# Fewer, larger transfers around the second layer of a graph network: kept rows by pairs, slot numbers by groups, segment marks by a product with a 0-1 matrix

## The chip, the core and the metric

The kernel runs on one core of a Trainium2 chip. Its time is the device time of one execution in microseconds (us); the time before is a median over four runs. Profile rows name the engines PE (TensorE matmul), PEld (its weight loads), DVE (VectorE), ACT (ScalarE), POOL (GpSimd) and SP (SyncE); SPq is SP's queue of transfers. In this kernel every plain transfer of the two long loops is issued by SP, in program order, and every indirect gather by POOL, in program order.

## The reference

A graph of 6250 nodes with 256 features and 106250 edges, sorted by destination; each node has one edge to itself. There are two layers, each followed by a residual and a layernorm.

```python
# layer 0
msgs = relu(relu(S @ W_r.T + b_r) @ W_r.T + b_r)       # S = feat[src], r = the edge's relation (0 or 1)
agg  = segment_sum(msgs, dst)
i, f, g, o = split(agg @ W_ih.T + b_ih + b_hh, 4)
hn   = sigmoid(o) * tanh(sigmoid(i) * tanh(g))
x    = layernorm(x + relu(relu(hn @ W1.T + b1) @ W2.T + b2) @ W3.T + b3)
# layer 1, four heads of 64 features
h    = (x @ W).reshape(n, 4, 64)
e    = leaky_relu(a_src[src] + a_dst[dst], 0.2)
ex   = exp(e - segment_max(e, dst)[dst])
out  = segment_sum(h[src] * ex / (segment_sum(ex, dst)[dst] + 1e-16), dst) + bias
x    = layernorm(x + relu(layernorm(out + x) * gamma + beta))
```

The inputs are those of `setup_inputs()`: float32 features and weights, int32 indices.

## The kernel before

**Tiling.** The self edges are taken out of the list, which leaves 100000 edges in TC = 782 tiles of P = 128. Seven tiles (WT) make a window (112 of them); the destinations of a window fit in 64 node slots. Two windows make a group (NG = 56), whose 128 slots fill the 128 partitions. Layer 1 works on pairs of groups: groups 0 to 51 in 26 pairs, the last four alone. Layer 0 does its update for two pairs (four groups) at a time up to group 47, then for pairs and for single groups.

**Layer 0.** The two-layer edge network depends on the source node and the relation only, so it is computed once for each node and relation and stored to DRAM (`parts`). For each tile POOL gathers 128 of these rows (helper `gather`, L1720), and PE sums them by slot with a one-hot matrix (L2162). `update()` (L1976 to L2127) then does the gates, the three-layer network, the residual and the layernorm of its groups, projects the result to `h` with the attention terms (`hr`, L2090), and writes two things to DRAM through SP: the rows that layer 1 gathers (L2097, two stores per group), and for each group a tile of 128 x 768 floats (`keep3`: projected rows, a copy made by ACT at L2091, and what layer 1's end needs), stored as `kept` at L2107. `keep3` is a ring of six tiles.

**Layer 1.** The first 21 tiles (EARLY) need rows that are not yet stored when they are gathered; `complete()` adds them by a one-hot product (L2272 to L2285). For the others POOL gathers rows from `rows`, up to a look-ahead that is largest at the start of the layer and shrinks to eight tiles (AHEAD1): `Pace.hold` lets a gather wait for a given DVE instruction. For each pair:

- `ahead()` (L2292 to L2342) loads with SP the slot number of every edge, broadcast from a DRAM table over the 64 partitions of each half (`dB`, L2301, two transfers of 128 KB for each group), and the segment marks (`cut`, L2308, one transfer of 30 KB for each group: 60 partitions of 129 floats, in which each tile's row stands four times, once for each head). Eight steps later it compares dB with the partition's own number (`ohT`, L2315), multiplies with the node terms (`pn`, L2319) and reduces (`of`, L2336).
- `weights()` (L2344 to L2397) adds, turns the logits on PE (L2359), runs segmented scans on DVE in which `cut` holds the bounds (L2366 and L2367), brings together segments that cross tiles (L2370 to L2374, with ACT's copy `ends` at L2372), scans again, turns back (L2382) and takes the exponential. PE's turns and small products share a ring of two PSUM buffers, `turn`.
- `weighted()` (L2399 to L2416) builds the one-hot tiles (L1826) and the weighted rows (L2405, L2410, L2411), and `sum1()` (L2498 to L2528) sums them on PE (L2526). At a group's first tile it loads the group's kept rows (`k3`, L2516, a ring of three).
- `finish()` (L2418 to L2491) divides, applies both layernorms with `k3`, and stores the output (L2477).

**What sets the order.** The program is written out by hand: functions are chains that yield a number of steps (class `Steps`), the main loop (L2547 to L2587) moves each chain on by one step per tile, and so the order on each engine and in each queue is the order of these steps. `aheads()` (L2530) starts `ahead()` of a pair about one pair before `weights()` of it, so its loads go out in SP's queue beside stores of outputs and loads of kept rows.

Of the kernel before, what the change touches and what calls it, by code (L numbers as in the profile page):

```python
# [33 lines left out]
F32 = mybir.dt.float32  # L34
# [8 lines left out]
P = 128  # L43
# [39 lines left out]
BLOCK1, BLOCK2 = 33, 40  # L83
AHEAD_G = range(AHEAD_W // 2)
LATE = 3
AHEAD0 = 2 * WT
AHEAD1 = WT + 1
NOROW = NP + SLOTS - 1
# [656 lines left out]
def gnn_kernel(  # L745
# [47 lines left out]
    slots = dram.tile([NW, (WT + 1) * P], BF16, name="slots")  # L793
    cuts = dram.tile([(NC + 1) * CT, P], F32, name="cuts")
    srcs = dram.tile([EARLY, P], F32, name="srcs")
    kept = dram.tile([NG, P, 3 * D], F32, name="kept")
    packed = dram.tile([2 * BLOCKS, HB], I32, name="packed")

    const = ctx.enter_context(tc.tile_pool(name="fconst", bufs=1))
# [844 lines left out]
def fast(  # L1644
# [46 lines left out]
    def at(ap, offset, dims):  # L1691
        return bass.AP(tensor=ap.tensor, offset=ap.offset + offset, ap=dims)
# [9 lines left out]
    def windows_of(g):  # L1702
        return range(2 * g, 2 * g + 2)
# [67 lines left out]
    def half_of(w):  # L1771
        return slice(SLOTS * (w % 2), SLOTS * (w % 2 + 1))
# [68 lines left out]
    with (  # L1841
# [134 lines left out]
        def update(groups, aT):  # L1976
# [62 lines left out]
            mv = ring(up, [P, 4, 2], F32, "fmv", 3)  # L2039
            rstd = ring(up, [P, 4], F32, "frstd", 3)  # L2040

            keep3 = [ring(up, [P, 3, D], F32, "keep3", 6) for g in groups]
            for i, g in enumerate(groups):
                u = everyone
                p3 = ring(upp, [P, 4 * P], F32, "fpg", 5)[:, : 2 * P]
# [34 lines left out]
            for i, g in enumerate(groups):  # L2080
                u = everyone
                ph = ring(upp, [P, 4 * P], F32, "fpg", 5)[:, : D + 2 * H]
                for k in range(2):
                    nc.tensor.matmul(  # L2084
                        ph[u, :], hs[i][:, k, u], Wx[:, k, :], start=(k == 0), stop=(k == 1)
                    )
                hr = ring(up, [P, D + 2 * H], F32, "hr", 3)
                if g >= NG - LATE:
                    hr = rows_l[:, g - (NG - LATE), :]
                nc.scalar.copy(hr[u, :], ph[u, :])  # L2090
                nc.scalar.copy(keep3[i][u, 2, :], ph[u, :D])  # L2091

                in_order(stored, g)
                for w in windows_of(g):
                    if w in at_w:
                        to = rows1[bass.ds(at_w[w], SLOTS), :]
                        keep_row(g, nc.sync.dma_start(to, hr[half_of(w), :HA]))  # L2097
                if g == NG - 1:
                    move = nc.gpsimd.indirect_dma_start(
                        out=rows1,  # L2100
                        out_offset=bass.IndirectOffsetOnAxis(ap=tail_i, axis=0),
                        in_=hr[:, :HA],
                        in_offset=None,
                    )
                    keep_row(g, move)
                yield 1
                nc.sync.dma_start(kept[g, u, :], keep3[i][u, :, :].rearrange("p c f -> p (c f)"))  # L2107

                nd = ring(up, [P, 2, H], F32, "nd", 3)
                left = ring(up, [P, 2, H], F32, "left", 3)  # L2110
                nd3 = ring(up, [P, 3, 2, H], BF16, "nd3", 3)
                nc.vector.tensor_copy(nd[u, 0, :], hr[u, HA : HA + H])  # L2112
                nc.vector.tensor_copy(nd[u, 1, :], hr[u, D:HA])
                lg = loop[u, g, :]
                nc.vector.tensor_add(lg, nd[u, 0, :], nd[u, 1, :])
                n3 = [nd3[u, c, :, :] for c in range(3)]
# [12 lines left out]
        got, ohs, sums, turned, stored, loop0, rows_x = {}, {}, {}, {}, [], {}, {}  # L2129
        run.start(weights_of_logits())  # L2130

        def order_of(g):
# [113 lines left out]
    with (  # L2246
# [40 lines left out]
        def tiles_in(g):  # L2287

            t0 = 2 * WT * g
            return range(t0, min(t0 + 2 * WT, TC)), range(t0, min(t0 + GS, TC))  # L2290

        def ahead(pair, box):  # L2292

            cut = ring(ep, [P, P + 1], F32, "cut", 3)
            of = ring(ep, [P, 2 * GS, 2 * H], F32, "of", 3)
            box.update(cut=cut, of=of)
            dBs = []
            for g in pair:
                dB = ring(ep, [P, W8, P], BF16, "dB", 3)
                for w in windows_of(g):  # L2300
                    nc.sync.dma_start(  # L2301
                        dB[half_of(w), :, :].rearrange("p j e -> p (j e)"),
                        at(slots, w * W8 * P, [[0, SLOTS], [1, W8 * P]]),
                    )
                dBs.append(dB)
            for i, g in enumerate(pair):
                n = len(tiles_in(g)[1])
                nc.sync.dma_start(  # L2308
                    cut[i * GS * H : (i * GS + n) * H, :],
                    at(cuts, tiles_in(g)[0][0] * P, [[P, n], [0, H], [1, P + 1]]),  # L2310
                )
            yield 8
            for i, (g, dB) in enumerate(zip(pair, dBs)):
                ohT = ring(ep, [P, W8, P], BF16, "ohT", 2)
                nc.vector.tensor_scalar(ohT, dB, slot_p, None, op0=OP.is_equal)  # L2315
# [26 lines left out]
                yield 1  # L2342

        def weights(pair, box):  # L2344
# [10 lines left out]
                return ap.rearrange("p (t h) -> p t h", h=H)  # L2355

            yield 1
            pe = ring(tps, [P, P], F32, "turn", 2)
            nc.tensor.transpose(pe[:rs, :], ef, ident)  # L2359
            yield 1  # L2360
            s1 = ring(ep, [P, P], F32, "s1", 2)
# [7 lines left out]
            pd = ring(tps, [P, P], F32, "turn", 2)  # L2369
            nc.tensor.matmul(pd[:rs, 0:1], toward[:rs, 0, :rs], b[:, P - 1 : P], start=True, stop=True)  # L2370
            nc.tensor.matmul(pd[:rs, 1:2], toward[:rs, 1, :rs], b[:, 0:1], start=True, stop=True)
            nc.scalar.copy(ends[:rs, :], pd[:rs, 0:2])  # L2372
# [8 lines left out]
            pm = ring(tps, [P, P], F32, "turn", 2)  # L2381
# [36 lines left out]
        def finish(g, ps):  # L2418
# [1 line left out]
            u = everyone  # L2420
            n = u.stop
            at_w = lows_of(ws)
            k3 = k3s[g]
            sm = ring(fp, [P, 4, H], F32, "sm", 3)
            w_own, den = sm[u, 0, :], sm[u, 1, :]
            nc.vector.tensor_sub(w_own, loop[u, g, :], ps[u, HA:])
# [71 lines left out]
        def sum1():  # L2498
# [12 lines left out]
            if g not in sums:  # L2511
                sums[g] = ring(eps, [P, D + 2 * H], F32, "fps1", 2)
                left[g] = len(tiles_in(g)[1])
                u = everyone
                k3s[g] = ring(fp, [P, 3, D], F32, "k3", 3)
                nc.sync.dma_start(k3s[g][u, :, :].rearrange("p c f -> p (c f)"), kept[g, u, :])  # L2516
            begins = left[g] == len(tiles_in(g)[1])
            left[g] -= 1
            j = t - 2 * WT * g
# [14 lines left out]
                yield from ahead(pair, boxes[pair[0]])  # L2534


        shift = ep.tile([P, 2, P], F32, name="shift")
        own_q = ep.tile([P, 2], F32, name="own_q")
        nc.vector.tensor_scalar(own_q, own_n[:, LATE - 2 :], float(N - P), None, op0=OP.subtract)
        for q in range(2):  # L2540
            nc.vector.tensor_scalar(
                shift[:, q, :], iota_f, own_q[:, q : q + 1], None, op0=OP.is_equal
            )
        run.start(aheads())
        pace = Pace(0)
        t = 0
# [103 lines left out]
```

## Time and profile before

| what | value |
|---|---|
| median of four runs | 2797.2 us (2789.18 to 2802.23) |
| profiled execution | 2816.18 us, span 2814.4 us, mean granted clock of TensorE 0.747 |
| layer 0's even part | about 200 to 1500 us of the span |
| layer 1's even part | about 1582 to 2790 us of the span |
| stores of kept rows | 56 of 384 KB |
| loads of kept rows | 56 of 384 KB |
| loads of slot numbers | 112 of 128 KB |
| loads of segment marks | 56 (55 of 30.2 KB, one of 24.2 KB) |

A row of the profile's first part reads: engine, busy us, share of the span, instructions. A group's row reads: line, engine, operation, output and input names, shapes, count, then busy us and mean ns of one, then the idle time in front of it with what ended most of that. In the chain that ended last each step leads back to what released it; "another core or an unknown queue" (or "remote") is a wait whose releaser the records do not show. A row of the waits reads: engine and line, what it waited for, us in all, times, longest us. A row of the timeline reads: start us, length us, engine, line, operation, output and input, and in square brackets the wait in front of it. A window's row reads: from and to, length, busy us and count of PE, PEld, DVE, ACT and POOL, granted clock, mean busy share of the 16 DMA engines, GB/s.

### The profile page before, as it was taken

To read this page: it belongs to the slowest core of one execution; us is meant where nothing else is said; L and a number is where in the kernel's file an instruction comes from. 1 tells how busy PE (TensorE), PEld (TensorE's weight loads), DVE (VectorE), ACT (ScalarE), POOL (GpSimd) and SP (SyncE) were. 2 spreads that over 40 slices of the span, in tenths; PEclk is the share of its full clock that TensorE was granted. 3 is DMA by queue.
4 is the path that set the end of the run, shared out by engine and by line. 5 is a ranking of instruction groups with operands and counts; after the bars stand their busy time and mean duration, and the time that the engine had idled before them with its cause. 6 is when DMAs were issued, how large, how long until landed. Compare 5 with 4: busy or idle time off the path is not lost. (4 is left out here: it accounts for less than half of the span.)

```text
span 2814.4 us, 23466 instructions
## 1 busy us (share of the span) xinstructions
PE 1574.7 (56%) x5945; PEld 822.3 (29%) x5945; DVE 1282.9 (46%) x3508; ACT 503.9 (18%) x1571; POOL 1527.9 (54%) x1610
## 2 busy tenths in 40 slices
PE   8855776575766766667744634534334342524354
PEld 5533433232322323323422412212222121212122
DVE  8542232322322322323322566755656565656576
ACT  3312021111111111112222011111111111111112
POOL 1253656665656565665544545556565655556561
PEclk9977888887878888788876756666666666656676
DMA  4333534444433443444434334435343444444441
GB/s 145 115 108 110 154 111 128 126 126 126 132 109 116 131 137 113 126 119 132 139 102 115 100 98 123 122 107 135 100 134 98 130 114 121 123 115 122 113 129 52
DMA packets 164626, 334.53 MB, mean 119 GB/s; under 512 B 42657, under 2 KB 75156, under 8 KB 164481
## 3 DMA queue, kind: packets, MB, share of 16 engines
q0 software_dynamic: 76048, 207.99, 27.5%
q1 hardware_dynamic: 86257, 121.90, 14.1%
q10 hardware_dynamic: 2176, 3.05, 0.4%
q8 instruction: 49, 0.80, 0.1%
q14 instruction: 96, 0.79, 0.1%
HBM read 280.25 MB, written 52.53 MB: 118 GB/s over the span
## 5 line engine op out<-in xcount | busy, mean ns | idle before, releaser
L1720 POOL DMA_INDIRECT G<-rows,fidx x761 | 725.7, 954 | 531.0 <-issue 160.9
L1720 POOL DMA_INDIRECT G<-parts,fidx x722 | 692.4, 959 | 487.4 <-issue 217.1
L2526 PE MATMUL fps<-gw,oh 128*64 128x264 f32 (+1 forms) x1674 | 431.8, 462 | 253.2 <-DVE gw L2411 251.7
L2162 PE MATMUL fps<-G,oh 128*64 128x257 f32 (+1 forms) x1674 | 465.0, 429 | 128.4 <-ACT G L2211 109.3
L2526 PEld LDWEIGHTS fps<-gw,oh 128*64 128x64 f32 (+1 forms) x1674 | 222.4, 164 | 419.0 <-DVE gw L2411 270.0
L2162 PEld LDWEIGHTS fps<-G,oh 128*64 128x64 f32 (+1 forms) x1674 | 204.0, 153 | 373.0 <-issue 184.2
L2411 DVE TENSOR_TENSOR gw<-G,bank 128x1792 f32<-128x1792 f32 (+1 forms) x167 | 249.0, 1491 | 63.0 <-ACT gw L2410 45.5
L2001 PE MATMUL fpg<-faT,fWihT 128*128 128x512 f32 (+2 forms) x432 | 187.1, 553 | 22.4 <-issue 16.9
L2382 PE MATMUL turn<-fident,s 120*128 120x120 f32 (+2 forms) x30 | 13.2, 439 | 294.0 <-DVE sm L2432 238.3
L2112 DVE COPY nd<-hr 128x4 f32<-128x4 f32 x53 | 9.6, 180 | 298.1 <-ACT hr L2090 226.1
L1826 DVE TENSOR_TENSOR oh<-bank,fslot 128x1024 f32<-128x1024 f32 x106 | 128.9, 1216 | 10.8 <-ACT bank L2390 6.8
L1575 PE MATMUL fpm<-fWrT,fhT 128*128 128x256 f32 x392 | 101.6, 413 | 12.2 <-DVE fms L1583 7.5
L1609 POOL DMA_INDIRECT G<-parts,fidx x60 | 57.0, 950 | 91.2 <-DMA parts<-fms 73.5
L2001 PEld LDWEIGHTS fpg<-faT,fWihT 128*128 128x128 f32 x432 | 75.4, 202 | 98.7 <-issue 88.0
L1919 DVE TENSOR_SCALAR kind<-fps 128x1 f32<-128x1 f32 x112 | 12.3, 151 | 198.8 <-PE fps L2162 173.8
L1561 PE MATMUL fph<-fxc,fWrT 128*128 128x512 f32 (+1 forms) x208 | 93.8, 600 | 10.7 <-ACT fhT L1568 5.8
L2460 ACT ACTIVATE frs<-fmv,eps_c 128x1 f32<-128x1 f32 x112 | 33.0, 294 | 360.6 <-DVE gw L2405 162.3
L2382 PEld LDWEIGHTS turn<-fident,s 120*128 120x128 f32 (+2 forms) x30 | 5.3, 177 | 298.8 <-DVE sm L2432 240.8
L1575 PEld LDWEIGHTS fpm<-fWrT,fhT 128*128 128x128 f32 x392 | 79.0, 207 | 34.8 <-issue 13.4
L2014 DVE TENSOR_TENSOR fgg<-fgg,fgi 128x512 f32<-128x512 f32 (+2 forms) x36 | 20.5, 571 | 144.5 <-ACT fgg L2009 111.0
L2466 ACT ACTIVATE fy<-fy,frs 128x256 f32<-128x256 f32 x112 | 66.8, 596 | 87.4 <-DVE gw L2405 51.0
L2084 PE MATMUL fpg<-Wx,fyT 128*128 128x264 f32 x224 | 77.1, 474 | 7.7 <-ACT fyT L2075 3.0
(347 smaller groups left out, 1993.3 us busy)
## 6 DMA issues: line engine op xcount, KB each, us to landing
kept<-keep SPq DMA_DIRECT2D x56, 384.0 KB
k<-kept SPq DMA_DIRECT2D x56, 384.0 KB
dB<-slots SPq DMA_DIRECT2D x112, 128.0 KB
loop<-parts SPq DMA_DIRECT2D x110, 128.0 KB
parts<-fms SPq DMA_DIRECT2D x49, 256.0 KB
G<-parts,fidx POOLq DMA_INDIRECT x782
G<-rows,fidx POOLq DMA_INDIRECT x761
fxn<-in_x_dram SPq DMA_DIRECT2D x110, 64.0 KB
```

The source lines that it names most:

```text
L1561: nc.tensor.matmul(ph[:, :cols], WrT_s[:, r, k, m * P : (m + 1) * P], xc[:, k, :cols], start=(k == 0), stop=(k == 1),)
L1575: made = nc.tensor.matmul(pm[:, r, :], hT[:, r, k, j * P : (j + 1) * P], WrT_s[:, r, k, :], start=(k == 0), stop=(k == 1),)
L1609: nc.gpsimd.indirect_dma_start(out=of[:, n % WT, :D], out_offset=None, in_=parts0[: 2 * P * block, :], in_offset=bass.IndirectOffsetOnAxis ...
L1720: return nc.gpsimd.indirect_dma_start(out=to_tile, out_offset=None, in_=table, in_offset=bass.IndirectOffsetOnAxis(ap=idx, axis=0),)
L1826: nc.vector.tensor_tensor(to[:, :nj, :], iota_s[:, None, :].to_broadcast([P, nj, SLOTS]), of[:, :, None].to_broadcast([P, nj, SLOTS]), op= ...
L2001: nc.tensor.matmul(pg[:, :cols], WihT_s[:, k, c * P : (c + 1) * P], aT[:, k, :cols], start=(k == 0), stop=(k == 1),)
L2084: nc.tensor.matmul(ph[u, :], hs[i][:, k, u], Wx[:, k, :], start=(k == 0), stop=(k == 1))
L2162: nc.tensor.matmul(sums[g][to, :], ohj, got[t], start=begins, stop=ends)
L2411: nc.vector.tensor_mul(gw[:, :, :D].rearrange("p j (h f) -> p j h f", h=H), of[:, :n, :D].rearrange("p j (h f) -> p j h f", h=H), ex[:, o ...
L2460: nc.scalar.activation(r, mv[u, k, 1:2], AF.Ln, bias=eps_c[u])
L2466: nc.scalar.activation(y, y, AF.Identity, bias=m, scale=r)
L2526: nc.tensor.matmul(sums[g][to, :], ohj, gw, start=begins, stop=ends)
```

## The change

Kept rows of two groups go in one transfer: the DRAM tensor `kept` gets the shape pairs x 128 x 2 x 768, so that both groups' rows of a partition lie side by side. In `update()` the ring of six tiles becomes one of three pair tiles, and the store goes out once per pair, after the odd group's row stores (56 stores become 30; the four single groups keep their own). In `sum1()` the ring of three becomes two pair tiles, loaded at the first tile of the even group (56 loads become 30).

The slot numbers of a group come in one transfer of 128 partitions, whose source has an outer step of two windows, 64 repeats and 1024 numbers (112 loads become 56).

The segment marks are loaded once, ahead of layer 1's loop: `cut_all`, 113 partitions x 7 chunks x 129 floats, row r of chunk c being tile 112 c + r (CR = 16 x 7 = 112). `pick` is a matrix of 0 and 1, 113 x 4 x 120, made by eight DVE operations. In `ahead()` PE multiplies the pair's columns of `pick` with its chunk of `cut_all`, which picks each tile's row and repeats it four times; the product goes into the `turn` ring, whose buffers become 129 columns wide, and ACT copies it to `cut`. This stands in the step that issues the loads, ahead of the `yield 8`.

```diff
-    kept = dram.tile([NG, P, 3 * D], F32, name="kept")
+    kept = dram.tile([NG // 2, P, 2, 3 * D], F32, name="kept")
...
-            keep3 = [ring(up, [P, 3, D], F32, "keep3", 6) for g in groups]
+            for g in groups:
+                if g % 2 == 0:
+                    kept_of[g // 2] = ring(up, [P, 2, 3, D], F32, "keep3", 3)
+            keep3 = [kept_of[g // 2][:, g % 2, :, :] for g in groups]
...
-                nc.sync.dma_start(kept[g, u, :], keep3[i][u, :, :].rearrange("p c f -> p (c f)"))
+                if len(groups) == 1:
+                    nc.sync.dma_start(
+                        kept[g // 2, :, g % 2, :], keep3[i].rearrange("p c f -> p (c f)")
+                    )
+                elif g % 2:
+                    nc.sync.dma_start(
+                        kept[g // 2], kept_of[g // 2].rearrange("p i c f -> p i (c f)")
+                    )
...
-                dB = ring(ep, [P, W8, P], BF16, "dB", 3)
-                for w in windows_of(g):
-                    nc.sync.dma_start(
-                        dB[half_of(w), :, :].rearrange("p j e -> p (j e)"),
-                        at(slots, w * W8 * P, [[0, SLOTS], [1, W8 * P]]),
-                    )
+                dB = ring(ep, [P, W8 * P], BF16, "dB", 3)
+                nc.sync.dma_start(
+                    dB, at(slots, 2 * g * W8 * P, [[W8 * P, 2], [0, SLOTS], [1, W8 * P]])
+                )
                 dBs.append(dB)
+            o = pair[0] % 2 * GS * H
+            n = ((len(pair) - 1) * GS + len(tiles_in(pair[-1])[1])) * H
+            pc = ring(tps, [P, P + 1], F32, "turn", 2)
+            nc.tensor.matmul(
+                pc[:n, :],
+                pick[:, pair[0] % 8 // 2, o : o + n],
+                cut_all[:, pair[0] // 8, :],
+                start=True,
+                stop=True,
+            )
+            nc.scalar.copy(cut[:n, :], pc[:n, :])
+            yield 8
             for i, g in enumerate(pair):
-                n = len(tiles_in(g)[1])
-                nc.sync.dma_start(
-                    cut[i * GS * H : (i * GS + n) * H, :],
-                    at(cuts, tiles_in(g)[0][0] * P, [[P, n], [0, H], [1, P + 1]]),
-                )
-            yield 8
-            for i, (g, dB) in enumerate(zip(pair, dBs)):
                 ohT = ring(ep, [P, W8, P], BF16, "ohT", 2)
-                nc.vector.tensor_scalar(ohT, dB, slot_p, None, op0=OP.is_equal)
+                nc.vector.tensor_scalar(
+                    ohT.rearrange("p j e -> p (j e)"), dBs[i], slot_p, None, op0=OP.is_equal
+                )
...
-            pe = ring(tps, [P, P], F32, "turn", 2)
+            pe = ring(tps, [P, P + 1], F32, "turn", 2)[:, :P]
...
-            k3 = k3s[g]
+            k3 = k3s[g // 2][:, g % 2, :, :]
...
-                k3s[g] = ring(fp, [P, 3, D], F32, "k3", 3)
-                nc.sync.dma_start(k3s[g][u, :, :].rearrange("p c f -> p (c f)"), kept[g, u, :])
+                if g % 2 == 0:
+                    k3s[g // 2] = ring(fp, [P, 2, 3, D], F32, "k3", 2)
+                of = k3s[g // 2].rearrange("p i c f -> p i (c f)")
+                if len(pair_of[g]) == 1:
+                    nc.sync.dma_start(of[:, g % 2, :], kept[g // 2, :, g % 2, :])
+                elif g % 2 == 0:
+                    nc.sync.dma_start(of, kept[g // 2])
...
+        pick = ep.tile([CR + 1, 4, 2 * GS * H], F32, name="pick")
+        for q in range(4):
+            row_q = ep.tile([P, 1], F32, name=f"row_{q}")
+            nc.vector.tensor_scalar(row_q, iota_p, float(4 * WT * q), None, op0=OP.subtract)
+            nc.vector.tensor_scalar(
+                pick[:, q, :].rearrange("p (i t h) -> p i t h", i=2, h=H),
+                bass.AP(
+                    tensor=iota_f.tensor,
+                    offset=iota_f.offset,
+                    ap=[[iota_f.ap[0][0], CR + 1], [2 * WT, 2], [1, GS], [0, H]],
+                ),
+                row_q[: CR + 1],
+                None,
+                op0=OP.is_equal,
+            )
...
+        cut_all = ep.tile([CR + 1, -(-TC // CR), P + 1], F32, name="cut_all")
+        nc.sync.dma_start(
+            cut_all, at(cuts, 0, [[P, CR + 1], [CR * P, -(-TC // CR)], [1, P + 1]])
+        )
         run.start(aheads())
```

More of the change, by code (lines that the diff above doesn't have):

```diff
@@ L85 @@
 LATE = 3
+CR = 16 * WT
 AHEAD0 = 2 * WT
@@ L2129, in fast @@
         got, ohs, sums, turned, stored, loop0, rows_x = {}, {}, {}, {}, [], {}, {}
+        kept_of = {}
         run.start(weights_of_logits())
@@ L2298, in ahead @@
             for g in pair:
-                dB = ring(ep, [P, W8, P], BF16, "dB", 3)
-                for w in windows_of(g):
-                    nc.sync.dma_start(
-                        dB[half_of(w), :, :].rearrange("p j e -> p (j e)"),
-                        at(slots, w * W8 * P, [[0, SLOTS], [1, W8 * P]]),
-                    )
-                dBs.append(dB)
+                dB = ring(ep, [P, W8 * P], BF16, "dB", 3)
+                nc.sync.dma_start(
+                    dB, at(slots, 2 * g * W8 * P, [[W8 * P, 2], [0, SLOTS], [1, W8 * P]])
+                )
+                dBs.append(dB)
+            o = pair[0] % 2 * GS * H
[10 more added lines that the diff above has]
+            yield 8
             for i, g in enumerate(pair):
-                n = len(tiles_in(g)[1])
-                nc.sync.dma_start(
-                    cut[i * GS * H : (i * GS + n) * H, :],
-                    at(cuts, tiles_in(g)[0][0] * P, [[P, n], [0, H], [1, P + 1]]),
-                )
-            yield 8
-            for i, (g, dB) in enumerate(zip(pair, dBs)):
-                ohT = ring(ep, [P, W8, P], BF16, "ohT", 2)
-                nc.vector.tensor_scalar(ohT, dB, slot_p, None, op0=OP.is_equal)
+                ohT = ring(ep, [P, W8, P], BF16, "ohT", 2)
+                nc.vector.tensor_scalar(
+                    ohT.rearrange("p j e -> p (j e)"), dBs[i], slot_p, None, op0=OP.is_equal
+                )
                 yield 2
@@ L2368, in weights @@
             yield 1
-            pd = ring(tps, [P, P], F32, "turn", 2)
+            pd = ring(tps, [P, P + 1], F32, "turn", 2)[:, :P]
             nc.tensor.matmul(pd[:rs, 0:1], toward[:rs, 0, :rs], b[:, P - 1 : P], start=True, stop=True)
@@ L2380, in weights @@
             yield slow
-            pm = ring(tps, [P, P], F32, "turn", 2)
+            pm = ring(tps, [P, P + 1], F32, "turn", 2)[:, :P]
             nc.tensor.transpose(pm[:, :rs], b, ident[:rs, :rs])
```

## The prediction

> **What bounds the kernel now.** The page comes first: no engine is near its span, and the chain that ended last holds little.
>
> ```profile
> PE 1574.7 (56%) x5945; PEld 822.3 (29%) x5945; DVE 1282.9 (46%) x3508; ACT 503.9 (18%) x1571; POOL 1527.9 (54%) x1610
> DMA  4333534444433443444434334435343444444441
> DVE 10%; another core or an unknown queue 5%; issue 3%; ACT 2%; PE 0%; POOL 0%; DMA 0%; DVEq 0%; ACTq 0%; POOLq 0%
> ```
>
> So no share of the whole decides; the stage does. The windows of layer 0 (first), the seam (second) and layer 1 (third) follow; the columns are length, then busy us (count) of PE, PEld, DVE, ACT and POOL, granted clock, DMA share, GB/s.
>
> ```profile
> 200.00:1500.00 1300.00, 868.76 (x2888) 410.03 (x2888) 379.37 (x1242) 254.57 (x660) 741.25 (x774) 0.82 0.42 123
> 1506.00:1582.00 76.00, 38.67 (x143) 29.10 (x143) 17.21 (x41) 3.32 (x10) 44.51 (x48) 0.71 0.48 133
> 1582.00:2790.00 1208.00, 495.01 (x2262) 272.03 (x2262) 744.50 (x1881) 182.55 (x765) 684.15 (x718) 0.65 0.43 116
> ```
>
> Layer 1 is where most of the change lies. It repeats once per pair of groups, at a median of 45.6 us (from the starts of the L2372 copies). Windows cut along one such period:
>
> ```profile
> 2294.90:2326.00 31.10, 16.25 (x70) 8.59 (x70) 25.62 (x63) 6.66 (x28) 18.36 (x20) 0.72 0.42 114
> 2326.00:2340.30 14.30, 1.39 (x12) 1.24 (x12) 1.38 (x6) 0.00 (x0) 8.26 (x9) 0.50 0.47 131
> 2340.30:2371.40 31.10, 16.04 (x70) 8.42 (x70) 25.58 (x63) 6.63 (x28) 18.32 (x20) 0.72 0.41 111
> ```
>
> 31.1 us are DVE's (25.6 busy, 82%). For 14.3 us PE, DVE and ACT stand still and only POOL's gathers go on. The timeline shows how that ends: ACT's copy L2372 had waited 14.35 us on a semaphore with no recorded cause. The waits of the same line give its size over the layer.
>
> ```profile
> 2340.35 0.16 ACT L2372 COPY ends<-turn 120x2 f32<-120x2 f32 x1 [14.35 <-remote]
> ```
>
> ```profile
> ACT ends L2372 <- remote: 293.8, 22, 14.8
> ```
>
> The waits of SP's own queue show what SP does meanwhile:
>
> ```profile
> SPq L2477 <- ACT gw L2410: 552.6, 25, 30.1
> SPq L2301 <- DVE G L2285: 37.5, 1, 37.5
> SPq L2516 <- DMA k<-kept: 9.4, 9, 1.4
> ```
>
> In that stand-still PE has its matmuls recorded by 2327.6, yet its semaphores come 4 to 13 us late; it ends some 2 us after the last packet of the gathers, when POOL has run out of look-ahead. I can't name the cause, only where it sits: 10 to 12 us after POOL starts to issue a gather every 1.25 us. In the first pair it comes (17.3 us) with none of SP's loads in flight, so these are not its sole cause. SP itself waits 552.6 us for values to store.
>
> **The change part by part.** The sum is made against the profiled execution (span 2814.4, time 2816.2 us) and is then moved to the median of the runs, 2797.2 us, which is 0.68% lower. Forms and rows are those of the trace.
>
> Kept rows, stores: 56 become 30 (26 pairs, four groups alone), same bytes. Each issue holds SP 0.51 us, and SP mostly waits. The even group's store now goes behind the odd group's two row stores, so behind SP's wait for ACT's L2091, met once in this trace (3.5 us); queued behind it on SP are the next groups' loads. The ring stays at six groups. Cost 0; the bounds are 6 us per double pair either way over 13 of them (periods of 84 to 91 us in layer 0 differ by about that), so -78 to +78, and I take 0 because issue and wait are near 0.
>
> Kept rows, loads: 56 become 30, the odd group's 384 KB now ride with the even group's. A 3,072-byte packet takes 121 ns; 384 KB are 8 of these on each of 16 engines, 1 us. The pair's load waits for the same finished group as the even one did. Cost 0.
>
> Slot numbers (dB): 112 transfers become 56, bytes equal. SP issues 0.60 us each, 33 us saved beside 552.6 us of waiting: 0. What matters is how the new form spreads. The old one fills 64 partitions; the new one fills 128 from a source of two outer steps with 64 repeats. The packet records of the index loads at the start of the trace show other shapes: the 126-row loads ran with up to 14 packets at once, a 125-partition one with 4.9 to 5.3, the 74-partition ones with 2.2 to 2.5. So the count of the outer step, not the bytes, sets how many engines work, and an outer step of 2 is nearest to the last row. I take 2 engines: 64 packets x 84 ns = 5.4 us for one dB, and as gathers hold about 40% of an engine at their 1.25 us spacing (0.50 us each), 5.4/0.6 = 9 us. With 2.2 us before the first packet, the pair's first dB lands about 11 us after issue, the second 20; at the pace inside the busy burst 14 and 26. The kernel before:
>
> ```profile
> 2319.28 2.42 SPq L2301 DMA_DIRECT2D dB<-slots  x4
> 2321.74 1.86 SPq L2308 DMA_DIRECT2D cut<-cuts  x2
> ```
>
> ```profile
> 2326.61 0.48 DVE L2315 TENSOR_SCALAR ohT<-dB,slot_p 128x1024 bf16<-128x1024 bf16 x1
> 2344.88 0.47 DVE L2315 TENSOR_SCALAR ohT<-dB,slot_p 128x1024 bf16<-128x1024 bf16 x1
> ```
>
> DVE uses the first dB 7.3 us after the first issue, the second 25.6 after. A first wait of 4 to 7 us falls on DVE just before the stand-still, which ends 21.1 us after issue, so it lies inside it: 0. The operations queued behind it on DVE are the scans and the one-hot products, and PE and ACT wait for those; they now wait anyway. The second is at 20 to 26 against 25.6: 0.5 us x 26 pairs = +13. Bounds: 0 if spread over 16 engines; if the cover goes, 5.5 us x 26 = +143.
>
> The Trainium skill, "DMA: Bandwidth & Descriptors", section "Why a DMA increments its semaphore by 16 and not by 1", takes the number of engines as the largest divisor up to 16 that both sides' slowest dimensions share, which speaks against this change: 2 for dB, 1 for a 113-row load. The three rows above agree (126: 14, 125: 5, 74: 2). By the rule the sum is the one below; by bytes at 16 engines it would be +5. The page's section "Rules for kernel authors" also says to coalesce small transfers into a large one; by that alone the sum would be negative by SP's issue time, and SP's 552.6 us of waiting says that nobody wants this time.
>
> Marks (cut): 56 loads of 30 KB and 0.88 us on SP go: 49 us of an idle queue, 0. In their place stands one load of 113 partitions x 7 pieces of 516 B at the seam. 113 has no divisor, so by the rows I take one engine: 791 x 33 ns = 26 us, over 0.6 = 43.5, plus 2.2: from about 1507 to 1553. It is issued ahead of dB, whose first ohT came at 1553.52:
>
> ```profile
> 1553.52 0.48 DVE L2315 TENSOR_SCALAR ohT<-dB,slot_p 128x1024 bf16<-128x1024 bf16 x1
> ```
>
> PE's new product waits for it, and the sums of the early tiles (L2278) stand behind it on PE; ACT's new copy waits for the product, and ACT's copies of e (L2571, L2579) behind that. dB of the first pair follows on its engines, to about 1562: +9. Bounds: 0 if spread, +30 at 44 ns a piece.
>
> Product and copy per pair: one fp32 matmul of 129 columns (like L2382, 0.44 us, or twice that for its greater height) and an ACT copy (0.27 to 0.37 us): 30 x 0.17 us on the path, as PE idles 3.3 us near it: +5 (0 to +20). It takes a turn more in a ring of two PSUM buffers, released by that copy. The 0-1 matrix: eight DVE operations, some 1.8 us, inside a DVE wait of 4.7 us at the seam: 0.
>
> Sum: 0 + 0 + 13 + 9 + 5 = +27: about 2843 for a profile like this one, 2824 against the median.
>
> **The rivals.**
>
> Faster: a shorter stand-still. For it: it takes 294 us on L2372 alone, follows a burst with DMA at 0.88, and was 9 us in early pairs with a deeper look-ahead. Against it: the first pair has it without SP's loads. If fewer SP transfers in that burst bring 14.4 down to 9.8, 22 x 4.6 = -101, with the seam's +9: 2705; a band of 2650 to 2788.
>
> No change: the new forms spread like the old ones, or all of it lies in the stand-still; 2797, and 2789 to 2806. The 125- and 74-partition rows speak against it; the 14.3 us of cover for it. (About 0.3% is what a measurement of this kernel can tell from none.)
>
> Slower still: dB becomes the period's bound. The mechanism is the two engines carrying dB while out and kept rows follow in the same rings; from 26 us for both dBs on it shows. 5.5 us x 26 = +143 gives 2940, half of it 2870; a band of 2870 to 2960. For it speaks the pace in the burst, against it the 40% only that gathers need.
>
> **How the numbers follow.** The forecast +27 (own range 2806 to 2870) 0.45; faster 0.30; no change 0.10; dB exposed 0.15. The range of 2700 to 2910 leaves out the lower third of the faster case (0.11) and the upper half of the last (0.08). Faster by over 0.3% is 0.30 and 0.02 of the no-change case: 0.32; within: 0.08; slower: 0.45 + 0.15 = 0.60.
>
> **What would show it.** Right: DVE's wait at L2315 is by DMA dB, several us each; dB's packets run two at a time; the first pn products come after 1555; the stand-still at L2372 shortens by as much as DVE's wait grew. Wrong: dB lands within 4 us; the period falls under 44 us with the copy's wait at 9 us; or layer 0's periods change, where I have nothing. The prediction is most at risk from the stand-still, whose cause the trace does not show.

## The result, and the profile after

The changed kernel takes 2777.95 us (median of 39 runs, 2761.36 to 2797.33) against 2796.35 us before (60 runs, 2775.28 to 2820.43). The ratio is 0.9932, with a 95% interval of 0.9918 to 0.9947: the change is faster by 0.7%, where 2824 us had been forecast.

One fact is needed for all that follows. The chips on which this was run are of two kinds. On some the kernel before takes 2772 to 2797 us and has the stand-still of 14 us in each pair that the prediction describes; on others the same program takes 2183 to 2185 us and has none. The result above, and the two profiles of this and the earlier part, are of the first kind. The experiments fell on both, and the kind is named with each; every ratio is between runs on one chip.

The page of the changed kernel, its engines and its transfers (engine, busy us, share, instructions; then line, count, size):

```profile
PE 1579.7 (57%) x6005; PEld 824.8 (30%) x6005; DVE 1283.5 (46%) x3516; ACT 510.5 (18%) x1601; POOL 1521.9 (55%) x1610
DMA packets 152063, 333.18 MB, mean 120 GB/s; under 512 B 39309, under 2 KB 69251, under 8 KB 151920
...
kept<-keep SPq DMA_DIRECT2D x26, 768.0 KB
k<-kept SPq DMA_DIRECT2D x26, 768.0 KB
dB<-slots SPq DMA_DIRECT2D x56, 256.0 KB
```

The work on the engines is that of before and the little that the change adds (60 matmul records on PE, 30 copies on ACT, eight operations on DVE), and the transfers are as few as the diff says (beside the 26 there are four of 384 KB, each way). The windows of the changed kernel, by stage and then along one pair:

```profile
200.00:1500.00 1300.00, 861.47 (x2894) 407.44 (x2894) 380.22 (x1251) 255.94 (x664) 738.75 (x775) 0.81 0.42 123
1502.00:1576.00 74.00, 33.46 (x147) 26.58 (x147) 19.30 (x51) 2.35 (x9) 44.59 (x47) 0.72 0.48 136
1576.00:2764.00 1188.00, 515.36 (x2317) 280.53 (x2317) 744.70 (x1882) 189.00 (x794) 680.26 (x717) 0.66 0.43 116
```

```profile
2275.70:2307.00 31.30, 17.10 (x72) 8.84 (x72) 25.84 (x65) 6.90 (x29) 19.33 (x21) 0.72 0.43 114
2307.00:2321.00 14.00, 1.46 (x12) 1.25 (x12) 1.44 (x6) 0.04 (x2) 8.34 (x9) 0.50 0.48 124
```

The part of the pair that belongs to DVE is as long as before (31.3 us). The stand-still is there again, a little shorter: the median of the waits in front of ACT's copy `ends` went from 14.39 to 13.33 us in the eighteen steady pairs (the 6th copy to the 24th), and the mean period from 45.59 to 44.80 us. The sum of these waits without a recorded cause was 293.8 us before and is now:

```profile
ACT ends L2389 <- remote: 280.7, 22, 15.6
```

The profiled span went from 2814.4 to 2787.6 us, 26.8 us. Cut at the first dB issue and at the copies of `ends`: layer 0 -4.9, the seam up to the first copy -2.2 (76.4 to 74.2 us), the next five pairs -3.8, eighteen steady pairs -14.2, the rest -1.7. What lies ahead of the first dB issue scatters by more than 4.9 us between two profiles of one kernel (1465.0 us in `cut_only` and 1472.6 in `cut_only_2` below, on two chips), so nothing is read from it. Most of the gain, 18 us, is in layer 1's pairs.

### The profile page after: what moved, and what is told of

It reads as the page before. It is cut to its first block, busy times and chain, and to the rows that moved or that the text cites. A ratio compares the mean times of both kernels' runs of the same rounds, so it can differ in the third digit from the quotient of the medians.

```text
span 2787.6 us, 23291 instructions
## 1 busy us (share of the span) xinstructions
PE 1579.7 (57%) x6005; PEld 824.8 (30%) x6005; DVE 1283.5 (46%) x3516; ACT 510.5 (18%) x1601; POOL 1521.9 (55%) x1610
## 4 chain that ended last, share of the span: by engine, by line
PE 26%; DVE 24%; another core or an unknown queue 21%; issue 16%; ACT 5%; DMA 4%; SPq 2%; POOL 0%; DVEq 0%; POOLq 0%; ACTq 0%
PE fps L2174 10%; DVE gw L2428 5%; PE fpg L2002 5%; DVE oh L1827 3%; PE fpm L1576 2%; PE fph L1562 2%; PE fpg L2088 2%; DMA dB<-slots 1%; PE fpg L2050 1%; SPq L2312 1%; DVE fst L2475 1%; DVE of L2353 1%; ACT fy L2483 1%; PE fpg L1935 1%
## 5 line engine op out<-in xcount | busy, mean ns | idle before, releaser
L2548 PE MATMUL fps<-gw,oh 128*64 128x264 f32 (+1 forms) x1674 | 443.7, 457 | 250.6 <-DVE gw L2428 227.8
L1920 DVE TENSOR_SCALAR kind<-fps 128x1 f32<-128x1 f32 x112 | 12.3, 150 | 198.3 <-PE fps L2174 167.8
L2443 DVE TENSOR_TENSOR sm<-loop,fps 128x4 f32<-128x4 f32 x56 | 8.5, 152 | 198.5 <-remote 180.3
L2033 PE MATMUL fpg<-fz,fW2T 128*128 128x512 f32 (+2 forms) x36 | 23.9, 757 | 106.6 <-ACT fz L2030 106.6
```

Source lines behind the costliest of these rows:

```text
L2548: nc.tensor.matmul(sums[g][to, :], ohj, gw, start=begins, stop=ends)
```

## The experiments

**The parts one by one, on a chip with the stand-still.** Three kernels take one part of the change each into the kernel before; the fourth is the changed kernel with a shorter look-ahead. The edits:

```diff
# kept_only: from the change, kept / keep3 / k3 by pairs; dB and cut loads as before
# db_only:   from the change, this alone
-                for w in windows_of(g):
-                    nc.sync.dma_start(dB[half_of(w), ...], at(slots, w * W8 * P, [[0, SLOTS], [1, W8 * P]]))
+                nc.sync.dma_start(dB, at(slots, 2 * g * W8 * P, [[W8 * P, 2], [0, SLOTS], [1, W8 * P]]))
# cut_only:  from the change, cut_all, pick, the product pc and its copy; dB and kept as before
# after_ahead5: the whole change, and
-AHEAD1 = WT + 1
+AHEAD1 = WT - 2
```

> Only the kept rows go by pairs (stores 56 to 30, loads 56 to 30); slot numbers and marks as before. Theory A (the gain is a shorter stand-still in layer 1, won by fewer transfers in the burst of dB, marks and kept rows ahead of it): -3 to -8 us, ratio 0.997 to 0.999, period of a pair still 45.5 us. Theory B (the gain is the kept rows' own, in layer 0 and at the seam as in layer 1): -15 to -20 us, ratio 0.993 to 0.995, and the first pair's copy of ends comes some 7 us earlier. Theory C (my terms): 0, ratio 1.000.

> Only the slot numbers go in one transfer of 128 partitions a group; all else as before. Theory A: half of the gain, -8 to -12 us, ratio about 0.996. Theory B: 0, ratio 1.000. Theory C (my term, the second dB on two engines comes too late): +13 us, ratio 1.005. In all, dB's 2048-byte packets run about 1.6 at a time in place of 7.

> Only the marks: one load of 113 partitions at the seam, product and copy per pair; kept rows and slot numbers as before. Theory A: half of the gain, -8 to -12 us, ratio about 0.996. Theory B: 0, ratio 1.000. Theory C (my terms, +9 at the seam and +5 for product and copy): +14 us, ratio 1.005.

> The changed kernel with POOL's look-ahead in layer 1 at 5 tiles in place of 8 (AHEAD1). Theory that the stand-still ends when POOL has run its look-ahead dry: three gathers fewer at 1.25 us, 3.75 us less of stand-still in each of some 21 pairs, -79 us against the changed kernel, ratio to the kernel before 0.965. Rival, the stand-still has a length of its own (about 13 us) and gathers come late after it: 0 to +80 us, ratio 0.993 to 1.02.

Before: 2776.64 us (31 runs).

| kernel | us | ratio, 95% interval | mean period of a pair |
|---|---|---|---|
| kept_only | 2780.51 | 1.0027 (1.0000 to 1.0055) | 45.45 |
| db_only | 2769.43 | 0.9970 (0.9947 to 0.9992) | 45.18 |
| cut_only | 2766.35 | 0.9966 (0.9937 to 0.9994) | 45.03 |
| after_ahead5 | 2749.37 | 0.9897 (0.9862 to 0.9933) | 44.46 |

The kept rows gain nothing; theory B falls. The two loads ahead of the stand-still seem to share the gain, as theory A has it, but the intervals are as wide as the effects, and the last set below puts this in doubt. The shorter look-ahead gave less than a third of what was expected if the stand-still were as long as POOL's run: its waits are 12.3 us in place of 13.3, not 9.6. POOL still issues 17 gathers without a pause ahead of the end of 11 of the 18 steady stand-stills (17 or 18 ahead of 10 of them with 8 tiles), so the look-ahead does not set that number.

**The same parts, and what they are made of, on chips without the stand-still.** `db_cut` is the changed kernel with kept rows as before; `db_half` gives the kernel before dB in two transfers of 128 partitions by half the numbers (still two engines, and 112 transfers); `db_many` gives it four of 64 partitions by half the numbers (16 engines, 224 transfers); `after_spaced` lets POOL fill a 128 x 128 tile after each gather of the changed kernel.

```diff
# db_half
+                for s in range(0, W8 * P, W8 * P // 2):
+                    nc.sync.dma_start(dB[:, s : s + W8 * P // 2],
+                        at(slots, 2 * g * W8 * P + s, [[W8 * P, 2], [0, SLOTS], [1, W8 * P // 2]]))
# db_many
                 for w in windows_of(g):
+                    for s in range(0, W8, W8 // 2):
+                        nc.sync.dma_start(dB[half_of(w), s : s + W8 // 2, :]...,
+                            at(slots, (w * W8 + s) * P, [[0, SLOTS], [1, W8 * P // 2]]))
# after_spaced
+                nc.gpsimd.memset(space, 0.0)
```

> The changed kernel with the kept rows back in single groups: slot numbers in one transfer and the marks' product stay. The parts alone gave 0.9970 (slot numbers), 0.9966 (marks) and 1.0027 (kept rows). If they add: 0.9936 here, 18 us under the kernel before, and faster than the full change would be on this chip by the 0.27% of the kept rows. If the kept rows in fact do nothing: about 0.993, like the full change. If the first two share one gain: 0.996 to 0.997.

> The kernel before with the slot numbers of a group in two transfers, each of all 128 partitions and half of the numbers: as many transfers as before (112), bytes the same, 1 KB packets, and two engines for each as in the one-transfer form. If the gain of the slot numbers' part comes from its few engines (a thinner stream, and 2 completions for each transfer in place of 16): 0.997 as in that part alone, mean period of a pair 45.1 to 45.2 us. If it comes from fewer transfers: 1.000, 45.5 us.

> The kernel before with the slot numbers of a group in four transfers of 64 partitions and half of the numbers: 224 transfers in place of 112, bytes the same, 16 engines. If the number of transfers or of their completions (64 a pair before, 128 here; 4 in the changed kernel) sets the length of the stand-still: 0.4 us more in each pair, period 46.0 us, ratio 1.003 to 1.005. If neither does: 1.000, 45.5 us.

> The changed kernel with a 128 x 128 memset by POOL after each gather of layer 1, so that POOL issues a gather every 1.45 to 1.55 us in place of 1.25. If the stand-still comes from gathers issued too densely: it falls from 13.5 us to under 6, the period to what POOL needs (28 x 1.5 = 42 us), 50 us less than the changed kernel, ratio 0.975. If it only lasts until POOL has run dry, whatever its pace: 17 x 0.25 = 4 us more in each of 20 pairs, +80 us, ratio 1.02.

Measured against 2184.29 us (15 runs): `db_cut` 1.0461 (1.0444 to 1.0478), `db_half` 1.0558 (1.0539 to 1.0578), `db_many` 1.0005 (0.9996 to 1.0014), `after_spaced` 1.0455 (1.0439 to 1.0471). Twice as many transfers on 16 engines cost nothing; the same number as before on two engines costs 5.6%, some 122 us. `after_spaced` can't answer its question, since the stand-still that it was to shorten wasn't there. Three parts were then run alone, and the full change:

```diff
# after_again: the change, unaltered;  db_only_2, kept_only_2: as db_only, kept_only
# cut_16: cut_only, and
-        nc.sync.dma_start(cut_all, at(cuts, 0, [[P, CR + 1], [CR * P, -(-TC // CR)], [1, P + 1]]))
+        nc.sync.dma_start(cut_all[:CR, :, :], at(cuts, 0, [[P, CR], [CR * P, -(-TC // CR)], [1, P + 1]]))
+        nc.sync.dma_start(cut_all[CR : CR + 1, :, :], at(cuts, CR * P, [[P, 1], [CR * P, -(-TC // CR)], [1, P + 1]]))
```

> The changed kernel once more, unaltered. Where the kernel before has its stand-still of 14 us a pair (some 2780 to 2800 us): 0.993, as measured. Where it has none (2184 us, period of a pair 35 us): the costs of my sum lie open, seam about +28 us and each pair 2 to 4 us longer, ratio 1.045 to 1.05 like the change without the kept rows (1.0461).

> Only the marks' part, with its one load cut into 112 partitions and the one that is left, so that the large one has 16 engines. If the engines of that load are what it costs at the seam: seam as in the kernel before. Without a stand-still in the kernel before: 0.999 to 1.002. With it: 0.996, as the part with one engine had (0.9966), since there the seam was no loss.

> The slot numbers' part alone once more. With the stand-still: 0.997 as before. Without it: no cost at the seam, 2 to 4 us in each pair, +60 to +80 us, ratio 1.03 to 1.036.

> The kept rows' part alone once more. With the stand-still: 1.0027 as before. Without it: 0, ratio 0.999 to 1.001 (my term), or up to 1.005 if the larger stores of layer 0 hold up what stands behind them on SP.

Before: 2185.18 us (23 runs). The last three columns are from one profile of each kernel: first dB issue to first copy of `ends`, the five pairs after it, and the mean period of the eighteen steady ones.

| kernel | us | ratio, 95% interval | seam | five pairs | period |
|---|---|---|---|---|---|
| kept_only_2 | 2184.61 | 1.0001 (0.9992 to 1.0010) | 42.9 | 157.8 | 34.86 |
| cut_16 | 2187.30 | 1.0013 (1.0002 to 1.0024) | 44.2 | 157.9 | 34.79 |
| db_only_2 | 2267.79 | 1.0380 (1.0360 to 1.0400) | 45.7 | 171.2 | 38.43 |
| db_cut (set above) | 2284.66 | 1.0461 (1.0444 to 1.0478) | 73.5 | 169.8 | 37.90 |
| after_again | 2237.89 | 1.0246 (1.0229 to 1.0264) | 73.4 | 167.7 | 35.64 |

Without the stand-still the change costs 2.5%, less than the 4.5 to 5% that was expected of `after_again`. The kernel before has no profile on such a chip, and `kept_only_2`, which takes the same time (1.0001), stands in for it. The table says where the cost lies: 30 us at the seam and 10 + 18 x 0.78 = 24 us in the pairs, nearly all of the 54.6 us between the spans of `after_again` and `kept_only_2`. The waits show the pairs' part, first of `db_only_2`, then of `after_again`, last SP's own queue in `kept_only_2` and in `db_only_2`:

```profile
DVE ohT L2313 <- DMA dB<-slots: 136.6, 46, 5.3
PEld L2319 <- DVE ohT L2313: 80.8, 25, 5.4
```

```profile
DVE ohT L2330 <- DMA dB<-slots: 74.1, 44, 3.7
```

```profile
SPq L2488 <- DMA out_dram<-fy: 105.3, 80, 3.5
```

```profile
SPq L2477 <- DMA out_dram<-fy: 299.5, 69, 10.6
```

DVE waits for dB, PE waits for DVE behind it, and the stores of outputs that SP issues after dB queue behind it too (299.5 us of waits for such stores in place of 105.3). The timeline of `db_only_2` shows one pair of it:

```profile
1764.89 0.47 SPq L2477 DMA_DIRECT2D out_dram<-fy  x1
1765.41 0.58 SPq L2516 DMA_DIRECT2D k<-kept  x1
1766.60 1.31 SPq L2300 DMA_DIRECT2D dB<-slots  x2
1775.97 11.50 SPq L2477 DMA_DIRECT2D out_dram<-fy  x2
1778.55 0.48 DVE L2313 TENSOR_SCALAR ohT<-dB,slot_p 128x1024 bf16<-128x1024 bf16 x1 [5.28 <-DMA dB<-slots]
1786.17 0.49 DVE L2313 TENSOR_SCALAR ohT<-dB,slot_p 128x1024 bf16<-128x1024 bf16 x1 [2.53 <-DMA dB<-slots]
```

An output store and the odd group's kept rows stand ahead of dB. In the changed kernel those rows came with the even group's, 17 us earlier, and the first dB is there about 9 us after its issue in place of 10 to 12. This fits that kept rows by pairs, which do nothing alone (1.0001), take the period from 37.90 to 35.64 us once dB is slow: that is the difference between `db_cut` and `after_again`, measured on two chips of this kind. Why they do it is read from the traces and is not shown by a run.

**The parts with 16 engines.** Two kernels keep the transfers as few as in the change and give them back their engines. Each window's slot numbers stand eight times in DRAM, made by one more transfer early in layer 0, so that the outer step of a load is 16.

```diff
-    slots = dram.tile([NW, (WT + 1) * P], BF16, name="slots")
+    slots = dram.tile([9 * NW, (WT + 1) * P], BF16, name="slots")
...
+        nc.sync.dma_start(at(slots, NW * W8 * P, [[8 * W8 * P, NW], [W8 * P, 8], [1, W8 * P]]),
+                          at(slots, 0, [[W8 * P, NW], [0, 8], [1, W8 * P]]))
...
-                    dB, at(slots, 2 * g * W8 * P, [[W8 * P, 2], [0, SLOTS], [1, W8 * P]])
+                    dB, at(slots, (NW + 16 * g) * W8 * P, [[W8 * P, 16], [0, 8], [1, W8 * P]])
# db_16: this on db_only;  all_16: this on the whole change, and cut_16's two loads
```

> The whole change with both loads spread: the slot numbers of every window stand eight times in DRAM (one extra transfer early in layer 0), so that a group's single load has an outer step of 16; the marks' load is cut into 112 partitions and one. Transfers as few as in the change. If few engines are what the change costs, then without a stand-still: 0.999 to 1.003, in place of 1.0246, period 34.8 us. With the stand-still: 0.993 if its gain comes from fewer transfers, 1.000 if it comes from the slot numbers' thin stream.

> Only the slot numbers' part, 56 loads with 16 engines each. Without a stand-still: 0.999 to 1.002, in place of 1.038. With the stand-still: 0.997 if the gain of this part comes from fewer transfers, 1.000 if from fewer engines.

Without the stand-still, against 2183.48 us (21 runs): `db_16` 0.9989 (0.9979 to 1.0000), `all_16` 1.0027 (1.0016 to 1.0037). One load a group is harmless on 16 engines and costs 3.8% on two: its 256 packets of a pair run 7 at a time for 3.8 us, where those of `db_only_2` run 1.5 at a time for 14 to 17. The remaining 0.27% of `all_16` lies ahead of layer 1's pairs (first copy of `ends` at 1224.0 us, against 1218.6 in `db_16`; periods 34.80 and 34.87 us). `all_16` was not run on a chip with the stand-still.

**Back on chips with the stand-still.** `kept_db` is the change without the marks' part, `cut_only_2` that part alone; the last two were meant to be faster.

```diff
# kept_db: kept_only and db_only together;  cut_only_2: as cut_only
# db_16_ahead5: db_16, and AHEAD1 = WT - 2;  cut_16_ahead5: cut_16, and AHEAD1 = WT - 2
```

> Kept rows by pairs and slot numbers in one transfer (two engines); marks as before. Without a stand-still: the full change's 1.0246 less the 28 us of the seam, 1.012, well under the 1.038 of the slot numbers alone, if the kept rows by pairs take the odd group's load out of the way of the slot numbers; 1.038 if that is not so and the marks' part is what helps. With the stand-still: 0.997 to 1.000.

> The marks' part alone once more, its load on one engine. Without a stand-still: the seam's 28 us and nothing else, ratio 1.012 to 1.013, first pair's copy of ends at about 1246 us. With the stand-still: 0.9966 as before.

> A version meant to be faster than both: one load of slot numbers a group on 16 engines, all else as before, and POOL's look-ahead in layer 1 at 5 tiles in place of 8. Without a stand-still gathers come later against their use: 1.000 to 1.01. With it, one gather less is streamed while PE, DVE and ACT stand: 0.990 to 0.995.

> The version from the findings: the marks' part alone, its load on 16 engines, and POOL's look-ahead in layer 1 at 5 tiles in place of 8; slot numbers and kept rows as before. With the stand-still: the marks' 0.995 less the 0.35% that the shorter look-ahead gave in the changed kernel, 0.990 to 0.993; 0.998 if the gain of the marks' part hangs on the one engine of its load. Without a stand-still: 1.001 as with 8 tiles, or up to 1.01 if gathers then come too late.

Against 2776.31 us (25 runs): `kept_db` 1.0010 (0.9982 to 1.0037), `cut_only_2` 0.9947 (0.9912 to 0.9982), `db_16_ahead5` 0.9989 (0.9958 to 1.0020). Against 2771.83 us (17 runs): `cut_16_ahead5` 0.9921 (0.9894 to 0.9947). So the gain is in the main the marks' part: alone it gives 0.34% and 0.53%, and the other two together nothing (`kept_db`). The 0.30% that the slot numbers' part had alone in the first set does not show there; whether that part adds anything to the full change is not settled. `kept_db` fell on a chip with the stand-still, so its question for a chip without one stays unanswered, and `db_16_ahead5` missed the 0.990 to 0.995 that was expected of it. The waits of `kept_db` and of `cut_only_2`:

```profile
ACT ends L2383 <- remote: 296.4, 22, 14.8
...
ACT ends L2383 <- PE turn L2382: 46.3, 6, 19.9
```

```profile
ACT ends L2378 <- remote: 268.8, 21, 14.2
```

In the eighteen steady pairs the median wait in front of that copy is 14.34 us in `kept_db`, as in the kernel before (14.39), and 13.68 us in `cut_only_2` (13.70 in `cut_only`); the mean periods are 45.57 and 44.98 us. The sums of the two views differ by more, but 25 us of that are two waits for PE in the second and third pair, which shrank (from 19.9 to 5.0 and from 10.9 to 1.2 us) while these two pairs took no less time. The gain does not hang on the one engine of the marks' load: `cut_16_ahead5` has it with 16, and the short look-ahead that it also has gave next to nothing in `db_16_ahead5` (taking off even the 0.35% between `after_ahead5` and the change leaves 0.4%). That kernel is 0.8% faster than the one before with the stand-still, level with the change, and its marks' part was 0.13% slower without one (0.02 to 0.24%); with the short look-ahead it wasn't run there.

## Why the prediction was wrong, point by point

The direction failed. The rival "faster: a shorter stand-still" had the mechanism and a band (2650 to 2788 us) that holds the result, at a size that was four times too large: 14.4 us fell by 1.1, not by 4.6.

- **Marks, 56 loads that go, "0"**: the step that failed. Their going was put at nothing because SP's queue was idle, and only their replacement was counted, +9 at the seam and +5 for product and copy, +14 in all. Alone, the marks' part takes 10 and 15 us off (0.9966 and 0.9947), because the stand-still did not keep its length: 13.7 us in place of 14.4 with this part, 13.3 with the whole change. Without a stand-still the part gains nothing (`cut_16` 1.0013), so it isn't SP's time that it saves, and the price of SP's time was right.
- **Product and copy, "+5"**: hidden with the stand-still. Without one, `cut_16` costs 2.8 us in all (0.4 to 5.2), so the term was of the right size or too large.
- **Second dB, "+13"**: two engines was right (1.6 packets at a time, 13 to 16 us for a pair's two loads in place of 4), and so was the landing. But the cover was complete, and the term should have been 0: DVE idles 0 to 2.8 us in front of the first dB's use in a steady pair, just ahead of the stand-still, and not at all in front of the second's. The changed kernel uses the first dB 10.8 us after its issue and the second 26.0 us after, where the second was at 25.6 before:

```profile
2299.46 1.22 SPq L2312 DMA_DIRECT2D dB<-slots  x2
...
2310.22 0.49 DVE L2330 TENSOR_SCALAR ohT<-dB,slot_p 128x1024 bf16<-128x1024 bf16 x1 [2.56 <-issue]
...
2320.98 0.16 ACT L2389 COPY ends<-turn 120x2 f32<-120x2 f32 x1 [13.96 <-remote]
...
2325.49 0.45 DVE L2330 TENSOR_SCALAR ohT<-dB,slot_p 128x1024 bf16<-128x1024 bf16 x1
```

  Where the cover is gone, the part alone costs 83 us, inside the bound of 143 that was worked out for that, and by the mechanism of the slower rival.
- **Seam, "+9"**: one engine was right too. The load was issued at 1502.33 and PE's product came at 1537.81, 35.5 us later (45.7 had been estimated); SP's next issue was held for 30.0 us in between, which I hadn't counted. Still the seam got no longer. The first line is of the kernel before, the others of the changed one:

```profile
1546.19 0.43 DVE L2285 TENSOR_TENSOR G<-G,fps 128x260 f32<-128x260 f32 x1 [15.69 <-remote]
...
1502.33 0.18 SPq L2582 DMA_DIRECT2D cut_all<-cuts  x1
1502.56 47.08 SPq L2312 DMA_DIRECT2D dB<-slots  x4
...
1537.81 0.76 PE L2319 MATMUL turn<-cut_all,pick 113*120 113x129 f32 x2 [38.90 <-issue]
...
1548.65 0.48 DVE L2330 TENSOR_SCALAR ohT<-dB,slot_p 128x1024 bf16<-128x1024 bf16 x1
```

  The first dB was used 46.1 us after its first issue, as before (46.0). There the kernel before stood still as well: DVE's sums L2285 had three waits without a recorded cause, 32.3 us together, the longest 15.69 us, and that time was free to be waited in. Without a stand-still the same load costs 28 us (73.5 us in `db_cut` against 45.7 in `db_only_2`), and `cut_16` takes this away by engines alone. The upper bound of +30 was near that, but it does not come out of its own working: 44 ns a piece in place of 33 gives some +23.
- **Kept rows, 0**: right alone, on both kinds of chip (1.0027 and 1.0001). What was missed is that the odd group's load stands in the queues just ahead of dB, and matters once dB is slow.
- **The rule on engines** of the Trainium skill, "DMA: Bandwidth & Descriptors", section "Why a DMA increments its semaphore by 16 and not by 1" (the largest divisor up to 16 of both sides' slowest dimensions), foretold both counts, 2 and 1. The traces agree: 1.6 packets of dB at a time, 0.7 of the marks' load, and the number of 4-byte packets (last section). `db_16`, with an outer step of 16 and 7 packets at a time, agrees as well. By the rule the prediction would have been the same; what it can't say is whether anyone waits.

So the sum counted two costs that were real and hidden and one that is small, held the stand-still at its length, and gave 0.6 to a slower kernel. The cover was in the profile, 14 us in each pair. What the trace didn't show is that this cover belongs to the chip: with it the change is 0.7% faster, without it 2.5% slower.

What stays open: what makes the stand-still, and by which step the marks' part shortens it. It isn't the number of transfers alone, since in layer 1 slot numbers and kept rows take away more of them (56 and 26, against 55) and together gain nothing. Their completions alone do not order them either: the 4-byte packets in SP's queue number 13059 in `kept_db` and 14735 in `cut_only_2`, and the second is the faster. Whether gathers issued less densely would shorten the stand-still wasn't tried where there is one.

## What to carry to other kernels

Merging transfers can take their engines away: one load a group in place of two cost nothing with an outer step of 16 (0.9989) and 3.8% with an outer step of 2, where nothing hid it. Read the packets of the new load side by side with those of the old one, and if they run one or two at a time, restore the outer step (a table stored eight times did it here) before anything else is judged. A cost that lies inside a wait without a recorded cause is not paid, but it is not gone: ask how long the wait would have to be, and treat a change whose cost is hidden only there as one that may turn into a loss where the wait doesn't occur. Price the parts of a change alone and together, since one that does nothing by itself can move what stands ahead of another in a queue.

## What the chip showed that was not expected

- The same program takes 2772 to 2797 us on some chips and 2183 to 2185 us on others. Gathers are issued equally fast on both (one every 1.25 us, the median 4,160-byte packet 161 to 182 ns), and busy times of POOL and DVE agree within 1% (1522 to 1534 and 1281 to 1291 us, but for `after_spaced`, where POOL has more to do). What differs is the idle time: without the stand-still the waits in front of the copy `ends` are 1 to 2 us, and TensorE's mean granted clock is 0.81 to 0.84 in place of 0.75 to 0.76. The clock alone is not the reason: PE is busy for 1574.7 us in the kernel before and for 1547.9 us in `kept_only_2` on a chip without the stand-still, 27 us less, where the time differs by some 600.
- The stand-still of layer 1 is only about half of that difference. The first load of slot numbers goes out at 1459 to 1508 us on the first kind and at 1174 to 1178 us on the second. Layer 0 too has waits without a recorded cause on the first kind, 459 us over all engines in the kernel before, of which the largest two groups are shown here; none of the ten profiles of the second kind has such a wait in either layer.

```profile
ACT fz L2029 <- remote: 124.0, 7, 20.1
ACT hr L2090 <- remote: 72.3, 8, 11.6
```

- A load that goes through one engine holds up the queue that issued it: SP needed 30.0 us for the issue after the marks' load in the changed kernel (30.9 in `cut_only` and `after_again`). In `cut_16`, where the same pieces go in a load of 112 partitions and one of a single partition, the issue after the first took 0.9 us and the next 0.6.
- A transfer leaves one 4-byte packet for each engine that took part in it. The change lowers their number in SP's queue by 3348, from 15571 to 12223, which is what 16 engines for each transfer of kept rows and of slot numbers before, two for each of slot numbers now, 15 for each load of marks (12 for the last, shorter one) and one for the new one give. The same count comes out in `db_half` (14003: two engines for each of 112) and in `db_many` (17363: 16 for each of 224). Counting them tells how many engines a transfer had.
